# The first loads of a two-layer attention kernel: fetched once, in the order of need, with zero rows behind the first scores

## The chip, the cores and the metric

The kernel runs on one core of a Trainium2 chip. The metric is the device time of one execution in microseconds (us). Engines are named as in the profile: PE is TensorE, DVE is VectorE, ACT is ScalarE, POOL is GpSimd, SP is SyncE. SP, ACT and POOL can also issue DMAs, each from its own queue, in the order of its instructions.

## The reference

Four stages follow one another on x of 2 x 1024 tokens with 256 features, each of the form x = layernorm(x + stage(x)):

```python
# stage 1: grouped-query attention, 32 query heads, 8 key/value heads, head size 8
q, k, v = x @ Wq + bq, x @ Wk + bk, x @ Wv + bv      # 256, 64 and 64 columns
q, k = rope(q), rope(k)
att = softmax(causal(q @ k.T / sqrt(8)))              # per head, 1024 x 1024
y = (att @ v) @ Wo + bo
# stage 2: FFN with int8 weights: down(silu(gate(x)) * up(x)), 1024 hidden
# stage 3: gated delta rule, 16 heads of 128 x 128, with convolutions, gates and an output projection
# stage 4: FFN with the signs of the weights: (relu(x @ sign(up).T * up_scale) @ sign(down).T) * down_scale * output_scale
```

Only stage 1 and the loads at the start of the program are touched by the change.

## The kernel before

Matrices are multiplied in single-pass float32 (`F32R`), so each operand is split into a high part rounded to that type and a low part, the difference; `mm3` (lines 788 to 792) multiplies high by high, high by low and low by high. `sub_low` (line 738) makes a low part. A rounded high part comes either from a copy on the chip or from a DMA on POOL's queue that converts on the way.

Stage 1 works on batch b in two passes that run interleaved. `first_pass` (line 1191) projects queries and keys (`project`, line 988), applies rope by multiplying the projection and its turned copy with cosine and sine rows and adding them, splits the result and sends it through DRAM (`qds`, `kds`), from where `maxima` (line 1038) loads it in the layout of the scores: a query tile qT and a key tile kT of four groups with 32 rows each. 24 rows of a group hold parts of the heads, two take the negated row maxima later, and the others must be zero or hold a fixed pattern. `clear_rows` writes the zero rows of `qds` in DRAM (512 KB for a batch and a half of the query heads, in rows of 512 bytes, from a zeroed tile `zo`), `clear_keys` fills a key tile with the pattern `pat`. `maxima` computes scores and their row maxima; `second_pass` (line 1228) computes the scores again, exponentiates on ACT and multiplies by the values. Beside both passes `split_weights` (line 806) streams stage 3's weights through the chip and splits them: DMA on SP, high part on ACT (line 828), low part on POOL.

At the start (lines 894 to 986) the program loads the identity, four small vectors of scales and biases, the projection weights `wqkv` (704 columns) twice, once in full precision in two tiles `wf` on SP and once converted (`whi`) on POOL's queue, then for each half of batch 0's tokens x twice in the same way (`xf`, `x2h`), the rope rows, and the masks. Low parts are made on DVE. `xf` has one buffer, so the second half's load waits until the first half has been subtracted. The first key tile and one other are filled by ACT, the third by DVE; POOL clears the value and maxima tiles.

The order of the instructions on each engine is not the order of the text: a planner that works with estimated times at compile time chooses it from what is ready, by the place in the program. `after(later, earlier)` (line 794) makes an instruction come behind another in that plan, without a wait on the chip; `anchor["mm"]` is the score matmul traced last in `maxima`. Where an instruction has no such order and no inputs, it can be put far ahead of its place in the text.

Of the kernel before, what the change touches and what calls it, by code (L numbers as in the profile page):

```python
# [11 lines left out]
F32 = mybir.dt.float32  # L12
# [8 lines left out]
P = 128  # L21
B, T, E = 2, 1024, 256
NT = B * T // P
TB = T // P
HQ, HKV, D = 32, 8, 8
G = HQ // HKV
# [695 lines left out]
def tile_two_layers(ctx: ExitStack, tc: tile.TileContext, a, out):  # L722
# [5 lines left out]
    def load(pool, src, shape, dtype=F32, name=None, eng=None):  # L728
        t = pool.tile(shape, dtype, name=name, tag=name)
        (eng or nc.sync).dma_start(out=t, in_=src)  # L730
        return t
# [6 lines left out]
    def sub_low(eng, lo, full, hi):  # L738

        eng.tensor_sub(lo, full, hi)  # L740

    ident = load(const, a["c_ident"], [P, P], name="ident")
# [155 lines left out]
    nc.sync.dma_start(out=bab, in_=a["bab"])  # L898
    nc.vector.memset(zero, 0.0)
    nc.sync.dma_start(out=small[:, 4:5], in_=a["out_s"].partition_broadcast(P))  # L900
    nc.sync.dma_start(out=down_scale, in_=a["dn_s"])
    nc.vector.tensor_mul(down_scale, down_scale, small[:, 4:5].to_broadcast([P, 2]))
    nc.sync.dma_start(out=up_scale, in_=a["up_s"])
# [18 lines left out]
    def load_x(b, half):  # L922

        cols = slice(b * T + half * 512, b * T + half * 512 + 512)
        xf = work.tile([P, 2, 512], F32, name="xf", tag="xf", bufs=1)
        xh = gx.tile([P, 2, HT], F32R, name="x2h", tag="x2h")
        xl = gx.tile([P, 2, HT], F32R, name="x2l", tag="x2l")
        for d in (
            nc.sync.dma_start(out=xf, in_=xsrc[:, :, cols]), nc.gpsimd.dma_start(out=xh, in_=xsrc[:, :, cols])
        ):  # L930
            if b:
                after(d, anchor["mm"])
        for k in range(2):
            sub_low(nc.vector, xl[:, k, :], xf[:, k, :], xh[:, k, :])
        return xh, xl
# [3 lines left out]
    nc.gpsimd.dma_start(out=whi, in_=wsrc)  # L939
    for k in range(2):  # L940
        wf = work2.tile([P, NW], F32, name="wf", tag="es", bufs=4)
        nc.sync.dma_start(out=wf, in_=wsrc[:, k, :])
        sub_low(nc.vector, wlo[:, k, :], wf, whi[:, k, :])
    bqk = load(wat, a["bqk"], [P, 6], name="bqk", eng=nc.scalar)
    rope = wat.tile([P, 2, T], F32, name="rope", tag="rope")
    xcols = {0: []}
    for half in range(2):
        xcols[0].append(load_x(0, half))
        c = slice(half * 512, half * 512 + 512)
        nc.sync.dma_start(out=rope[:, :, c], in_=a["c_rope"][:, :, c])  # L950
    masks = wat.tile([P, 2, P], F32R, name="masks", tag="masks")
# [8 lines left out]
    pat = load(wat, a["c_pat"], [P, G], name="pat", eng=nc.scalar)  # L960
# [4 lines left out]
    def clear_rows(b, m):  # L965
        nc.scalar.dma_start(
            out=qds[b][m][:, :, 3 * D :, :].rearrange("k g r (n t) -> (k g) r n t", t=P),
            in_=zo.unsqueeze(1).to_broadcast([P, TB, P]),
        )

    clear_rows(0, 0)

    def clear_keys(t, copy):
        for g in range(G):
            copy(t[:, g, :], pat[:, g : g + 1].to_broadcast([P, T]))

    clear_keys(kTs[0], nc.scalar.copy)
# [7 lines left out]
    for t in mxs:  # L985
        nc.gpsimd.memset(t, -3e38)

    def project(b, m, half, xs):

        xh, xl = xs  # L990
        c0, nr = m * P, (P, P, 64)[m]
# [4 lines left out]
        for r in range(2):  # L996
            w0 = c0 + r * 320
            for k in range(2):
                n = P if r else nr
                mm3(pp[0:n, r, :], whi[:, k, w0 : w0 + n], wlo[:, k, w0 : w0 + n],  # L1000
                    xh[:, k, :], xl[:, k, :], k == 0, k == 1)
            t = work.tile([P, 512], F32, name="t", tag="t", bufs=4)
            nc.vector.scalar_tensor_tensor(
                t[0:nr], pp[0:nr, r, :], bqk[0:nr, 2 * m + r : 2 * m + r + 1], rope[0:nr, r, c], ALU.add, ALU.mult
            )
            tt.append(t)
# [159 lines left out]
    def residual(b):  # L1166

        if b == 0:
            wout["w"] = load(wout_pool, a["wo0"].rearrange("(k p) f -> p k f", p=P), [P, 2, E], name="wo0")
            wout["b"] = load_row(wout_pool, a["bo"], E, "bo")  # L1170
        after(nc.sync.dma_start(
            out=x[:, b * TB : (b + 1) * TB, :],
            in_=a["x"][b * T : (b + 1) * T, :].rearrange("(n p) e -> p n e", p=P),
        ), anchor["mm"])
        for n in range(TB):
            nc.gpsimd.tensor_add(x[:, b * TB + n, :], x[:, b * TB + n, :], wout["b"])
# [14 lines left out]
    def first_pass():  # L1191
        for b in range(B):
            if b == 0:
                for half in range(2):
                    for m in (2, 0):
                        project(b, m, half, xcols[b][half])
                    yield 0
                clear_keys(kTs[1], nc.scalar.copy)
                clear_keys(kTs[2], nc.vector.tensor_copy)
            for kv in range(HKV):  # L1200
# [9 lines left out]
                if b + 1 < B and kv >= NEXT:  # L1210
                    n, half = divmod(kv - NEXT, 2)
                    if n == 0 and half == 0:
                        xcols[b + 1] = [load_x(b + 1, h) for h in range(2)]
# [10 lines left out]
                for w in maxima(b, kv):  # L1224
                    yield w / 36
# [224 lines left out]
```

## Time and the profile before

| | |
|---|---|
| time of three runs | 2094.68 us median, 2094.62 to 2099.72 |
| the profiled execution | 2099.4 us, span 2097.7 us from its first to its last instruction |
| mean granted clock of TensorE | 0.973 |
| busy, share of the span | PE 91%, DVE 77%, ACT 54%, POOL 36% |
| DMA | 230.90 MB, mean 110 GB/s |
| first matmul of the scores | at 39.48 us |

The profile is one execution. A line of the timeline has the start in us, the duration in us, the engine, the line of the program, the operation, its output and inputs with partitions and elements, the count, and in brackets the idle time of the engine before it and what ended it. SPq and ACTq are the two engines' queues of DMA issues; the duration there is that of issuing, not of the transfer. A line of a table by stretches has, for each engine, busy time and the number of instructions, then the granted clock, the busy share of the 16 DMA engines, and GB/s.

### The profile page before, as it was taken

To read this page: it belongs to the slowest core of one execution; us is meant where nothing else is said; L and a number is where in the kernel's file an instruction comes from. 1 tells how busy PE (TensorE), PEld (TensorE's weight loads), DVE (VectorE), ACT (ScalarE), POOL (GpSimd) and SP (SyncE) were. 2 spreads that over 40 slices of the span, in tenths; PEclk is the share of its full clock that TensorE was granted. 3 is DMA by queue.
4 is the path that set the end of the run, shared out by engine and by line. 5 is a ranking of instruction groups with operands and counts; after the bars stand their busy time and mean duration, and the time that the engine had idled before them with its cause. 6 is when DMAs were issued, how large, how long until landed. Compare 5 with 4: busy or idle time off the path is not lost.

```text
span 2097.7 us, 48705 instructions
## 1 busy us (share of the span) xinstructions
PE 1905.9 (91%) x18656; PEld 1498.2 (71%) x18656; DVE 1611.1 (77%) x3878; ACT 1131.9 (54%) x2349; POOL 762.8 (36%) x1217
## 2 busy tenths in 40 slices
PE   4989999999988887899999999999999999999996
PEld 2545555555555786788888888888888888787885
DVE  5756666877747996587788878888898888978587
ACT  2355566576655345555555555655564565555543
POOL 1243333331123322144363443444345344344331
PEclk9899999999999899999999999999999999999999
DMA  7454443442132421443444444443444343443110
GB/s 222 144 164 144 144 131 126 142 134 68 51 75 61 133 64 35 127 126 91 119 121 115 124 118 115 107 120 107 121 131 119 113 118 107 137 118 107 32 41 31
DMA packets 313514, 230.90 MB, mean 110 GB/s; under 512 B 139649, under 2 KB 278657, under 8 KB 313281
## 3 DMA queue, kind: packets, MB, share of 16 engines
q1 hardware_dynamic: 299472, 210.80, 34.6%
q10 hardware_dynamic: 9632, 10.76, 1.6%
q0 software_dynamic: 4176, 6.23, 1.2%
q8 instruction: 147, 2.41, 0.5%
q14 instruction: 87, 0.70, 0.1%
HBM read 172.95 MB, written 51.87 MB: 107 GB/s over the span
## 4 chain that ended last, share of the span: by engine, by line
PE 50%; DVE 19%; ACT 6%; DMA 5%; issue 4%; SPq 1%; POOL 1%; POOLq 0%; DVEq 0%; ACTq 0%
PE pp L790 4%; PE pp L792 4%; PE pp L791 4%; PE ps L1110 4%; PE av L1131 3%; PE ps L1058 3%; DVE q L216 2%; PE pkq L404 2%; DVE at L247 2%; PE pw L529 2%; PE pm L541 2%; DVE k L216 2%; PE pkk L253 2%; PE po L555 2%; PE p L380 2%
## 5 line engine op out<-in xcount | busy, mean ns | idle before, releaser
L1067 DVE TENSOR_REDUCE mx<-ps 128x4 f32<-128x1024 f32 (+1 forms) x320 | 344.7, 1111 | 133.5 <-PE ps L1058 91.9
L1114 ACT ACTIVATE es<-ps 128x512 f32<-128x512 f32 (+1 forms) x608 | 314.8, 577 | 135.3 <-PE ps L1110 128.7
L1110 PE MATMUL ps<-qT,kT 128*128 128x512 f32 (+3 forms) x768 | 221.1, 369 | 17.9 <-ACT es L1114 15.8
L1058 PE MATMUL ps<-kT,qT 128*128 128x512 f32 x576 | 203.2, 428 | 23.3 <-DVE mx L1067 16.9
L1110 PEld LDWEIGHTS ps<-qT,kT 128*128 128x128 f32 x768 | 130.9, 189 | 106.2 <-ACT es L1114 53.7
L216 DVE SCALAR_TENSOR_TENSOR k<-pp,cw,k 128x511 f32<-128x511 f32 (+2 forms) x192 | 141.8, 740 | 31.0 <-ACT k L209 19.9
L1058 PEld LDWEIGHTS ps<-kT,qT 128*128 128x128 f32 x576 | 102.5, 194 | 85.7 <-DVE mx L1067 51.9
L1131 PE MATMUL av<-es,vaug 128*32 128x512 f32 (+3 forms) x1536 | 161.7, 501 | 0.0
L216 DVE SCALAR_TENSOR_TENSOR v<-pp,cw,v 128x511 f32<-128x511 f32 (+2 forms) x192 | 141.2, 738 | 13.1 <-ACT halos L213 8.5
L416 POOL TENSOR_TENSOR q<-q,dg 128x512 f32<-128x512 f32 x64 | 82.2, 1285 | 184.5 <-ACT pt L460 31.6
L216 DVE SCALAR_TENSOR_TENSOR q<-pp,cw,q 128x511 f32<-128x511 f32 (+2 forms) x192 | 139.2, 733 | 11.0 <-ACT q L209 9.4
L740 POOL TENSOR_TENSOR wfl<-wf,wfh 128x256 fp32r<-128x256 f32 x80 | 58.4, 733 | 208.3 <-ACT wfh L828 165.2
L1117 POOL TENSOR_SCALAR_AFFINE_SELECT es<-es 128x512 f32<-128x512 f32 x128 | 80.3, 636 | 146.9 <-ACT es L1114 146.7
L529 PE MATMUL pw<-prs,lt 128*128 128x128 f32 x512 | 84.8, 288 | 23.4 <-ACT prs L523 23.3
L555 PE MATMUL po<-wc,at 128*128 128x128 f32 x512 | 98.4, 279 | 2.1 <-ACT wc L531 1.2
L763 POOL TENSOR_TENSOR om<-om 128x8 f32<-128x8 f32 x93 | 20.3, 218 | 213.7 <-DVE om L756 113.8
L529 PEld LDWEIGHTS pw<-prs,lt 128*128 128x128 f32 x512 | 70.7, 194 | 33.2 <-ACT prs L523 29.7
L558 ACT COPY o<-po 128x256 f32<-128x256 f32 x128 | 47.6, 372 | 79.3 <-PE po L555 78.4
L242 POOL TENSOR_SCALAR_AFFINE_SELECT d<-col 128x512 f32<-128x512 f32 x64 | 51.2, 812 | 105.6 <-DVE at L247 96.7
L554 PE MATMUL po<-M,q 128*128 128x128 f32 x448 | 87.6, 278 | 0.0
L828 ACT CAST wfh<-wf 128x256 fp32r<-128x256 f32 x80 | 32.3, 406 | 101.6 <-DMA wf<-in_w1k 28.6
L531 ACT COPY wc<-pw 128x256 f32<-128x256 f32 x128 | 47.5, 371 | 72.7 <-PE pw L529 71.7
(305 smaller groups left out, 5646.1 us busy)
## 6 DMA issues: line engine op xcount, KB each, us to landing
da<-dec SPq DMA_DIRECT2D x64, 256.0 KB
wk<-w1k SPq DMA_DIRECT2D x64, 256.0 KB
wq<-w1q SPq DMA_DIRECT2D x64, 256.0 KB
wv<-w1v SPq DMA_DIRECT2D x64, 256.0 KB
dg<-dec SPq DMA_DIRECT2D x64, 256.0 KB
wg<-w1g SPq DMA_DIRECT2D x64, 256.0 KB
wo<-w1o SPq DMA_DIRECT2D x64, 256.0 KB
ad<-avs ACTq DMA_DIRECT2D x32, 256.0 KB
```

The costliest lines, as they stand in the source:

```text
L216: nc.vector.scalar_tensor_tensor(acc[:, d:], pp[:, 0 : HT - d], cw[:, n, hd, KS - 1 - d : KS - d], acc[:, d:], ALU.mult, ALU.add)
L529: nc.tensor.matmul(pw[:, r], lhsT=lt[:, h * HC + c, :], rhs=prs[:, r], start=True, stop=True)
L554: nc.tensor.matmul(po[:, r], lhsT=st[i]["q", h][:, t], rhs=M[:, r], start=True, stop=False)
L555: nc.tensor.matmul(po[:, r], lhsT=st[i]["at", h][:, t], rhs=wc[:, r], start=(M is None), stop=True)
L790: nc.tensor.matmul(out, lhsT=lhi, rhs=rhi, start=k0, stop=False)
L791: nc.tensor.matmul(out, lhsT=lhi, rhs=rlo, start=False, stop=False)
L792: nc.tensor.matmul(out, lhsT=llo, rhs=rhi, start=False, stop=k1)
L1058: anchor["mm"] = nc.tensor.matmul(ps[:, j - j0, :].rearrange("p (g k) -> p g k", k=P), lhsT=q_, rhs=kT[:, :, j * P : (j + 1) * P], start=T ...
L1067: nc.vector.tensor_reduce(mx[:, it, j0 // 2, :], ps[:, 0:n, :].rearrange("p j (g k) -> p g j k", k=P), AX.XY, ALU.max)
L1110: nc.tensor.matmul(ps[:, g - g0, :], lhsT=kT[:, g, jb * P : (jb + 1) * P], rhs=qT[:, i0 : i0 + w], start=True, stop=True,)
L1114: exps.append(nc.scalar.activation(es[:, g0 : g0 + n, 0:w], ps, AF.Exp, scale=D ** -0.5))
L1131: mm = nc.tensor.matmul(av[ROW * g : ROW * (g + 1), i0 - ih * 512 : 512], lhsT=vaugs[b][:, jb, kv, :], rhs=es[:, g, 0:w], start=(jb == 0), ...
```

## The change

Batch 0's x and the projection weights are no longer fetched a second time with conversion; their high parts are copied (and rounded) on ACT from the full-precision tiles. `load_x` and the new `load_w` issue the loads and return a function that does the splitting, which is called later. The columns of `wqkv` are arranged anew, keys and values first, and the first 192 of them come in a load of their own on ACT's queue. x is loaded first, on SP, in two pieces for a half. The second half is split when `first_pass` comes to it, behind the last rope multiplication traced before (`anchor["t"]`). The identity is loaded last. Zero rows for the first key/value head are written at the start, the others, and the loads of wo, bo and the small vectors, behind a score matmul. All three key tiles are filled by POOL, two of them behind POOL's other clearing. The product of the two scales goes from DVE to POOL.

```diff
@@ -739,7 +739,7 @@
 
         eng.tensor_sub(lo, full, hi)
 
-    ident = load(const, a["c_ident"], [P, P], name="ident")
+    ident = const.tile([P, P], F32, name="ident", tag="ident")
 
     def load_tokens(pool, n, count, bufs=1, tag="xtok"):
         t = pool.tile([P, count, E], F32, name="xtok", tag=tag, bufs=bufs)
@@ -895,12 +895,19 @@
     gx = open_pool(ctx, "gx", "right", 2)
     small = gx.tile([P, 2 * NF], F32, name="small", tag="small", bufs=1)
     bab, zero, down_scale, up_scale = small[0 : 2 * H, 0:1], small[:, 1:2], small[:, 2:4], small[:, NF:]
-    nc.sync.dma_start(out=bab, in_=a["bab"])
     nc.vector.memset(zero, 0.0)
-    nc.sync.dma_start(out=small[:, 4:5], in_=a["out_s"].partition_broadcast(P))
-    nc.sync.dma_start(out=down_scale, in_=a["dn_s"])
-    nc.vector.tensor_mul(down_scale, down_scale, small[:, 4:5].to_broadcast([P, 2]))
-    nc.sync.dma_start(out=up_scale, in_=a["up_s"])
+
+    def load_small():
+
+        for d in (
+            nc.sync.dma_start(out=bab, in_=a["bab"]),
+            nc.sync.dma_start(out=small[:, 4:5], in_=a["out_s"].partition_broadcast(P)),
+            nc.sync.dma_start(out=down_scale, in_=a["dn_s"]),
+            nc.sync.dma_start(out=up_scale, in_=a["up_s"]),
+        ):
+            after(d, anchor["mm"])
+        nc.gpsimd.tensor_mul(down_scale, down_scale, small[:, 4:5].to_broadcast([P, 2]))
+
     ones = gx.tile([H, P], F32, name="ones", tag="ones", bufs=1)
     nc.vector.memset(ones, 1.0)
     toks = open_pool(l0, "toks", "right")
@@ -925,29 +932,55 @@
         xf = work.tile([P, 2, 512], F32, name="xf", tag="xf", bufs=1)
         xh = gx.tile([P, 2, HT], F32R, name="x2h", tag="x2h")
         xl = gx.tile([P, 2, HT], F32R, name="x2l", tag="x2l")
-        for d in (
-            nc.sync.dma_start(out=xf, in_=xsrc[:, :, cols]), nc.gpsimd.dma_start(out=xh, in_=xsrc[:, :, cols])
-        ):
-            if b:
-                after(d, anchor["mm"])
-        for k in range(2):
-            sub_low(nc.vector, xl[:, k, :], xf[:, k, :], xh[:, k, :])
-        return xh, xl
+        if b:
+            after(nc.sync.dma_start(out=xf, in_=xsrc[:, :, cols]), anchor["mm"])
+            after(nc.gpsimd.dma_start(out=xh, in_=xsrc[:, :, cols]), anchor["mm"])
+        else:
+            for k in range(2):
+                nc.sync.dma_start(out=xf[:, k, :], in_=xsrc[:, k, cols])
+
+        def split():
+            for k in range(2):
+                if b == 0:
+                    d = nc.scalar.copy(xh[:, k, :], xf[:, k, :])
+                    if half:
+                        after(d, anchor["t"])
+                sub_low(nc.vector, xl[:, k, :], xf[:, k, :], xh[:, k, :])
+            return xh, xl
+
+        return split
 
     whi = wat.tile([P, 2, NW], F32R, name="whi", tag="whi")
     wlo = wat.tile([P, 2, NW], F32R, name="wlo", tag="wlo")
-    nc.gpsimd.dma_start(out=whi, in_=wsrc)
-    for k in range(2):
-        wf = work2.tile([P, NW], F32, name="wf", tag="es", bufs=4)
-        nc.sync.dma_start(out=wf, in_=wsrc[:, k, :])
-        sub_low(nc.vector, wlo[:, k, :], wf, whi[:, k, :])
-    bqk = load(wat, a["bqk"], [P, 6], name="bqk", eng=nc.scalar)
     rope = wat.tile([P, 2, T], F32, name="rope", tag="rope")
-    xcols = {0: []}
-    for half in range(2):
-        xcols[0].append(load_x(0, half))
+
+    def load_w(c, eng):
+        wf = work2.tile([P, 2, c.stop - c.start], F32, name="wf", tag="es", bufs=4)
+        eng.dma_start(out=wf, in_=wsrc[:, :, c])
+
+        def split():
+            nc.scalar.copy(whi[:, :, c], wf)
+            sub_low(nc.vector, wlo[:, :, c], wf, whi[:, :, c])
+
+        return split
+
+    def load_rope(half):
         c = slice(half * 512, half * 512 + 512)
         nc.sync.dma_start(out=rope[:, :, c], in_=a["c_rope"][:, :, c])
+
+
+    split_x = load_x(0, 0)
+    split_w = load_w(slice(0, 192), nc.scalar)
+    load_rope(0)
+    bqk = load(wat, a["bqk"], [P, 6], name="bqk", eng=nc.scalar)
+    pat = load(wat, a["c_pat"], [P, G], name="pat", eng=nc.scalar)
+    split_w()
+    xcols = {0: [split_x()]}
+    split_w = load_w(slice(192, NW), nc.sync)
+    split_w()
+    xcols[0].append(load_x(0, 1))
+    load_rope(1)
+    nc.sync.dma_start(out=ident, in_=a["c_ident"])
     masks = wat.tile([P, 2, P], F32R, name="masks", tag="masks")
     nc.gpsimd.dma_start(out=masks, in_=a["c_mask"])
 
@@ -957,24 +990,26 @@
     kTs = [big.tile([P, G, T], F32R, name=f"kT{i}", tag=f"kT{i}") for i in range(NKT)]
     zo = wat.tile([P, P], F32, name="zo", tag="zo")
     nc.vector.memset(zo, 0.0)
-    pat = load(wat, a["c_pat"], [P, G], name="pat", eng=nc.scalar)
     qds = [[dram.tile([4, G, ROW, T], F32, name=f"qd{b}{i}", tag=f"qd{b}{i}") for i in range(2)] for b in range(B)]
     ads = [[dram.tile([4, G, ROW, T], F32, name=f"ad{b}{i}", tag=f"ad{b}{i}") for i in range(2)] for b in range(B)]
     kds = [dram.tile([HKV, 3 * D, T], F32, name=f"kd{b}", tag=f"kd{b}") for b in range(B)]
 
-    def clear_rows(b, m):
-        nc.scalar.dma_start(
-            out=qds[b][m][:, :, 3 * D :, :].rearrange("k g r (n t) -> (k g) r n t", t=P),
-            in_=zo.unsqueeze(1).to_broadcast([P, TB, P]),
+    def clear_rows(b, m, kvs=slice(0, 4)):
+        n = (kvs.stop - kvs.start) * G * (ROW - 3 * D)
+        d = nc.scalar.dma_start(
+            out=qds[b][m][kvs, :, 3 * D :, :].rearrange("k g r (n t) -> (k g) r n t", t=P),
+            in_=zo[0:n].unsqueeze(1).to_broadcast([n, TB, P]),
         )
-
-    clear_rows(0, 0)
-
-    def clear_keys(t, copy):
+        if "mm" in anchor:
+            after(d, anchor["mm"])
+
+    clear_rows(0, 0, slice(0, 1))
+
+    def clear_keys(t):
         for g in range(G):
-            copy(t[:, g, :], pat[:, g : g + 1].to_broadcast([P, T]))
-
-    clear_keys(kTs[0], nc.scalar.copy)
+            nc.gpsimd.tensor_copy(t[:, g, :], pat[:, g : g + 1].to_broadcast([P, T]))
+
+    clear_keys(kTs[0])
     vaugs = [big.tile([P, TB, HKV, ROW], F32, name=f"vaug{i}", tag=f"vaug{i}") for i in range(B)]
     for t in vaugs:
         nc.gpsimd.memset(t, 0.0)
@@ -984,23 +1019,25 @@
     mxs = [wat.tile([P, TB, TB // 2, G], F32, name=f"mx{i}", tag=f"mx{i}") for i in range(NMX)]
     for t in mxs:
         nc.gpsimd.memset(t, -3e38)
+    for t in kTs[1:]:
+        clear_keys(t)
 
     def project(b, m, half, xs):
 
         xh, xl = xs
-        c0, nr = m * P, (P, P, 64)[m]
+        c0, nr = (192, 448, 0)[m], (P, P, 64)[m]
 
         c = slice(half * 512, half * 512 + 512)
         tt = []
         pp = ps_s.tile([P, 2, 512], F32, name="pp", tag="s")
         for r in range(2):
-            w0 = c0 + r * 320
+            w0 = c0 + r * nr
             for k in range(2):
                 n = P if r else nr
                 mm3(pp[0:n, r, :], whi[:, k, w0 : w0 + n], wlo[:, k, w0 : w0 + n],
                     xh[:, k, :], xl[:, k, :], k == 0, k == 1)
             t = work.tile([P, 512], F32, name="t", tag="t", bufs=4)
-            nc.vector.scalar_tensor_tensor(
+            anchor["t"] = nc.vector.scalar_tensor_tensor(
                 t[0:nr], pp[0:nr, r, :], bqk[0:nr, 2 * m + r : 2 * m + r + 1], rope[0:nr, r, c], ALU.add, ALU.mult
             )
             tt.append(t)
@@ -1166,8 +1203,11 @@
     def residual(b):
 
         if b == 0:
-            wout["w"] = load(wout_pool, a["wo0"].rearrange("(k p) f -> p k f", p=P), [P, 2, E], name="wo0")
-            wout["b"] = load_row(wout_pool, a["bo"], E, "bo")
+            wout["w"] = wout_pool.tile([P, 2, E], F32, name="wo0", tag="wo0")
+            wout["b"] = wout_pool.tile([P, E], F32, name="bo", tag="bo")
+            after(nc.sync.dma_start(out=wout["w"], in_=a["wo0"].rearrange("(k p) f -> p k f", p=P)), anchor["mm"])
+            after(nc.sync.dma_start(out=wout["b"], in_=a["bo"].partition_broadcast(P)), anchor["mm"])
+            load_small()
         after(nc.sync.dma_start(
             out=x[:, b * TB : (b + 1) * TB, :],
             in_=a["x"][b * T : (b + 1) * T, :].rearrange("(n p) e -> p n e", p=P),
@@ -1192,11 +1232,11 @@
         for b in range(B):
             if b == 0:
                 for half in range(2):
+                    if half:
+                        xcols[b][half] = xcols[b][half]()
                     for m in (2, 0):
                         project(b, m, half, xcols[b][half])
                     yield 0
-                clear_keys(kTs[1], nc.scalar.copy)
-                clear_keys(kTs[2], nc.vector.tensor_copy)
             for kv in range(HKV):
                 if kv == 1 and b == 0:
                     clear_rows(b, 1)
@@ -1210,7 +1250,7 @@
                 if b + 1 < B and kv >= NEXT:
                     n, half = divmod(kv - NEXT, 2)
                     if n == 0 and half == 0:
-                        xcols[b + 1] = [load_x(b + 1, h) for h in range(2)]
+                        xcols[b + 1] = [load_x(b + 1, h)() for h in range(2)]
                     if n < 2:
                         if half == 0:
                             clear_rows(b + 1, n)
@@ -1221,7 +1261,9 @@
                         else:
                             project(b + 1, 1, half, xs)
                             values(b + 1, half)
-                for w in maxima(b, kv):
+                for n, w in enumerate(maxima(b, kv)):
+                    if n == 0 and b == 0 and kv == 0:
+                        clear_rows(0, 0, slice(1, 4))
                     yield w / 36
                 yield 0
 
@@ -1408,7 +1450,7 @@
     arrays = {
         "x": x,
         "xT": x.T,
-        "wqkv": np.concatenate([wq, wk, turned(wq), turned(wk), l0("attn_Wv")], axis=1),
+        "wqkv": np.concatenate([wk, turned(wk), l0("attn_Wv"), wq[:, :P], turned(wq)[:, :P], wq[:, P:], turned(wq)[:, P:]], axis=1),
         "bqk": np.stack([bq[:P], turned(bq)[:P], bq[P:], turned(bq)[P:], pad(bk), np.concatenate([turned(bk), l0("attn_bv")])], axis=1),
         "wo0": l0("attn_Wo"),
         "bo": l0("attn_bo"),
```

## The prediction

> **What bounds the kernel now.** I read the page's head, then busy time by stretches, then the stretch 0 to 50 us in order of time, the waits of the DMA queues, and the DMA issues with their sizes. By stretches (busy us of each engine, granted clock, DMA share, GB/s):
>
> ```profile
> 0.00:20.00 20.00, 1.09 (x2) 0.39 (x2) 10.03 (x11) 8.94 (x9) 7.42 (x15) 1.00 0.92 274
> 20.00:40.00 20.00, 14.19 (x48) 9.32 (x49) 12.38 (x19) 3.85 (x6) 0.00 (x0) 1.00 0.54 183
> 40.00:50.00 10.00, 4.65 (x15) 2.44 (x14) 6.53 (x7) 0.26 (x1) 0.00 (x0) 0.94 0.66 179
> 50.00:60.00 10.00, 8.63 (x18) 4.41 (x17) 8.11 (x8) 0.74 (x3) 1.45 (x2) 0.50 0.76 241
> 100.00:200.00 100.00, 89.59 (x481) 49.76 (x484) 60.88 (x72) 55.52 (x116) 38.56 (x52) 0.98 0.45 141
> ```
>
> The kernel is a TensorE kernel (PE busy 91% of 2097.7 us) with an idle head: PE does 1.09 us of work in its first 20 us, while the DMA engines are 92% busy. Later it is 90% busy and more. The head in order of time:
>
> ```profile
> 10.32 4.17 ACTq L966 DMA_DIRECT2D qd<-zo  x2
> 14.04 0.38 SPq L929 DMA_DIRECT2D xf<-in_xT  x1
> 19.72 1.29 DVE L740 TENSOR_TENSOR x2l<-xf,x2h 128x512 fp32r<-128x512 f32 x2 [4.70 <-DMA xf<-in_xT]
> 20.46 0.69 PE L791 MATMUL pp<-x2l,whi 128*64 128x512 f32 x1 [8.23 <-DVE x2l L740]
> 25.50 1.29 DVE L740 TENSOR_TENSOR x2l<-xf,x2h 128x512 fp32r<-128x512 f32 x2 [0.58 <-DMA xf<-in_xT]
> 39.48 0.47 PE L1058 MATMUL ps<-kT,qT 128*128 128x512 f32 x1 [2.32 <-DMA qT<-qd]
> 49.25 2.04 PE L1058 MATMUL ps<-kT,qT 128*128 128x512 f32 x4 [3.77 <-DMA qT<-qd]
> ```
>
> The first projection waits for the low part of x (20.46), that for the full-precision copy of x (xf), and xf is only issued at 14.04. Why so late is in the DMA queue's own waits (us in total, times, longest), and what was in its way in the issues (count, KB each, us to landing):
>
> ```profile
> SPq L929 <- DMA qd<-zo: 7.9, 1, 7.9
> ```
>
> ```profile
> qd<-zo ACTq DMA_DIRECT2D x4, 512.0 KB
> x2h<-in_xT POOLq DMA_DIRECT2D x2, 512.0 KB, 9.9
> whi<-in_wqkv POOLq DMA_DIRECT2D x1, 704.0 KB, 6.4
> ```
>
> All four writes of zero rows (2048 KB) have been put at the very front, and xf stands behind one of them. With x and the weights fetched twice (x2h 1024, xf 1024, whi 704, wf 704), rope 1024, wo 256, masks and bo 128 each and ident 64, some 7.1 MB go out before 25 us. The microseconds 6 to 24 move 325 to 406 GB/s each; that is the head: 7.3 MB at about 370 is 19.7 us.
>
> **Part 1, loads up to the first low part.** Before it is done at 19.72 + 0.69 = 20.41 us. In the new order only half of x (512 KB) and 192 columns of weights (192 KB) must land, 0.72 MB or 1.9 us at 370 GB/s. The fixed part: the 2 KB of pat, issued at 1.25, landed at 3.35, so 2.1 us. Issue at 0.81 as now, plus 2.1, plus 1.9 is 4.8. The other bound is xf's own trip among other traffic, 5.6 us from 14.04: 0.81 + 0.4 for a second issue + 5.6 = 6.8. I take 5.8. The high parts are now rounded on ACT: 406 ns for 256 columns (wfh) and 620 for 512 (hi) put 384 at about 0.51, and x's first half at 0.62; with DVE's 0.69 for the low part this gives 5.8 + 0.51 + 0.62 + 0.69 = 7.6. ACT's table load (1.28) fits before the landing. **Gain 12.8 us** (11.8 to 13.8).
>
> **Part 2, from there to the first scores.** Before 39.48 - 20.41 = 19.1 us of projection, rope, splitting, and the trip through DRAM. That chain stays, but the second half's subtraction (1.29 at 25.50, after 0.58 of idling for xf) is now ordered behind the first half's rope multiplications. **Gain 1.9** (0 to 1.9). The second half keeps its place: its loads want the xf buffer free (about 8.3 us) and 4.5 us as now (issue at 21.04, subtraction at 25.50), so they land near 13, and its projections begin when the first half's are through. rope's first half and the remaining 512 KB of weights are issued behind x, and at 370 GB/s they add 2.8 us, to about 8.6: before the first rope product, which needs twelve matmuls at 0.43 after 6.9.
>
> **Part 3, what is added on GpSimd.** The patterns of the three key tiles (8 copies on ACT at 1.04, 4 on DVE) become 12 copies on GpSimd. Its nearest row is a cast of 128x512 in 612 ns, so 1.22 each, 14.7 us in all, beside memsets of 4.5 us that it does already. With pat landing at about 4.5, even the whole list ends near 24; the first key tile is written at about 34.18 - 13 = 21 and its four copies take 4.9. So GpSimd's own time is covered. Its neighbour is not: these rows (min/median/max ns first) show VectorE held by GpSimd:
>
> ```profile
> L1081 DVE TENSOR_TENSOR mp<-nm,mp x16: 187/200/426, 70.5 to 598.9; 128x32 fp32r<-128x32 f32 x16
> 70.12 0.73 POOL L740 TENSOR_TENSOR wfl<-wf,wfh 128x256 fp32r<-128x256 f32 x1 [3.06 <-ACT wfh L828]
> 70.48 0.43 DVE L1081 TENSOR_TENSOR mp<-nm,mp 128x32 fp32r<-128x32 f32 x1
> L975 DVE CAST kT<-pat x4: 675/680/5740, 3.3 to 10.2; 128x1024 fp32r<-128x1024 f32 x4
> ```
>
> The subtraction that takes 200 ns took 426 and ended with GpSimd's instruction (70.85 against 70.91); the cast of 680 took 5740 while GpSimd cleared memory. In the new head VectorE does eight two-input operations up to the first scores (two for weights, two for x, two sums, two low parts), so 0 to 8 x 1.22 = 9.8 us of waiting. Four lie on the chain (x twice, the queries' sum and low part), and an arrival in the middle of a copy waits half of it: 4 x 0.61. **Loss 2.4** (0 to 9.8).
>
> The Trainium skill (SBUF — State Buffer, section with the port table and "The single rule") speaks against the change here: a VectorE instruction with two inputs in SBUF and a GpSimd instruction that reads SBUF exclude each other for the whole instruction, while one that only writes does not. Taken at its word for all eight, each losing a full copy, the sum below would be a gain of 3.4 instead of 10.8; the row at 70.48 agrees with it for one case.
>
> **Part 4, what is moved into the running kernel.** Zero rows, three writes of 512 KB and one of 384, go to ACT's queue among the exponentials; ACT's busy share there is 56%. The nearest issue rows are 1.34 for two when the DMA engines are free (at 1.75 us) and 4.17 for two when full (10.32); bo's held the queue for 5.84. At the DMA share of 0.45 I take 0.65 each, 2.6 on ACT. In 40 to 200 us PE waits on ACT for 4.8 us only, so less than half arrives: **loss 1.0** (0 to 23.4 = 4 x 5.84). What is queued behind are exponentials, and PE's second pass waits for those. Four small loads (0.33 to 0.43 each), wo and bo go to SP behind the first scores, near the load of x at 103 us: SP idles 53 us for ACT's casts in 40 to 200, and wo is first read at 385 us, bo at 108.61 by GpSimd, which already waits 2.1 us for x there. Nothing. ident (first read at 72) and masks: nothing. The product for down_scale goes from DVE to GpSimd and waits there for its loads, with selects behind it that feed PE: **loss 0.5** (0 to 2.1, the fixed part of a load).
>
> **Sum.** -12.8 - 1.9 + 2.4 + 1.0 + 0.5 = -10.8 us. The profiled execution took 2099.4 us (span 2097.7 and 1.7 around it), 4.7 over the median of 2094.68 and inside the three runs (2094.62 to 2099.72). So 2088.6 for such an execution, and **2083.9** for the median. The gain can travel to the end, since nothing after the head has a date of its own: the weight stream, scores and exponentials start from the first scores. The instruction order is planned at compile time and can shift with the head; PE's idle time in 100 to 600 us is 31.7 us (10.4 + 15.7 + 5.6), and a third of it, 10 either way, is my estimate of that risk.
>
> **Rivals.**
> 1. *The head stays long for another reason.* VectorE loses every meeting with GpSimd (9.8): a gain of 3.4, 2091.3. For it: the cast of 5.74 us. Against: four of eight operations are off the chain and GpSimd also waits in its turn.
> 2. *Slower, by zero rows on ACT's queue.* If each issue is held like bo's, 23.4 us instead of 1.0 gives -11.8 + 23.4 = +11.6, 2106.3. It decides from 4.5 us an issue on (18.1 in all, +6.3). For it: the share of 0.76 in 50 to 60 us, and 512-byte rows. Against: 0.45 after 100 us.
> 3. *More is gained, by the clock.* In 50 to 60 us the granted clock is 0.50 (0.54 in 60 to 70), after PE idled 3.77 us at 49.25. VectorE is busy 8.11 and 8.26 of 10 there, so an unthrottled PE could give at most 3.6: 2080.3; with the planner's order on its side, 2072. For it: a smaller gap between the halves. Against: the second half still makes the same trip through DRAM. The Trainium skill (TensorE: Matmul & The Clock Gate, Part 1) has idle time of some 3.4 us put the clock at half. By that rule 0.4 us off the gap would be enough for this case.
> 4. *It doesn't do what it says:* the planner again puts zero rows in front of x. Then nothing is won in part 1 beyond the removed 1728 KB (4.8 us): 2090. The orders behind the score matmul speak against it. I count this with rival 1.
>
> **Chances.** A measurement of this kernel can tell about 0.3%, 6.3 us, from no change: faster is below 2088.4, slower above 2101.0. Forecast case 0.56; rival 3 (more) 0.16; rivals 1 and 4 (same) 0.17; rival 2 (slower) 0.11. So faster 0.72, same 0.17, slower 0.11. The range goes from rival 3's 2072 to 2096, which takes in rivals 1 and 4 with 5 us of planner's noise and leaves out rival 2 and a small tail below.
>
> **What would show it.** Right: xf issued at about 0.8; the first low part near 7.6; first scores near 27 (39.48 - 12.3) and the second half's near 37; the zero rows on ACT's queue after the first scores, each issue under 1 us; VectorE's subtractions in the head at 0.7 to 1.9 us; PE in 100 to 200 us (shifted by 11) still near 90%. Wrong: subtractions of 2 us and more (rival 1); issues of zero rows over 4.5 us with PE waiting on ACT behind them (rival 2); a head that is 11 us shorter with the end in its old place, which would mean that a later wait took it back.

## The result, and the profile after

| | before | changed |
|---|---|---|
| median of six runs each, us | 2094.65 (2091.54 to 2099.72) | 2115.83 (2107.58 to 2123.76) |
| ratio, 95% interval | | 1.0097, 1.0077 to 1.0116 |
| the profiled execution, us | 2099.4 | 2123.76 (span 2122.0) |
| mean granted clock | 0.973 | 0.962 |
| first scores, at us | 39.48 | 31.01 |

The changed kernel is 21 us slower; 11 us faster were forecast. Yet its head is shorter, by 8.5 us at the first scores (12.3 were predicted). Below are the stretches of the changed kernel (length; busy us and instructions of PE, PE's weight loads, DVE, ACT and POOL; granted clock; DMA share; GB/s). The last one runs from the first product of stage 3's keys and queries (called "stage 3's keys" below) to the last matmul of stage 4's first layer:

```profile
0.00:20.00 20.00, 10.18 (x25) 6.18 (x25) 7.90 (x12) 6.32 (x9) 18.12 (x23) 0.96 0.52 164
20.00:40.00 20.00, 12.96 (x39) 7.17 (x37) 14.71 (x19) 2.54 (x4) 1.33 (x2) 0.84 0.44 136
40.00:50.00 10.00, 3.81 (x8) 2.17 (x8) 2.87 (x3) 0.40 (x1) 0.72 (x1) 0.50 0.88 240
100.00:200.00 100.00, 93.42 (x544) 54.70 (x545) 64.00 (x74) 60.91 (x126) 44.28 (x60) 0.97 0.55 172
725.00:2109.20 1384.20, 1272.48 (x14924) 1120.33 (x14922) 1081.08 (x3108) 726.64 (x1538) 540.04 (x895) 0.97 0.35 100
```

The same stretch of the kernel before, whose code the change does not touch there:

```profile
738.60:2084.70 1346.10, 1250.71 (x14937) 1101.41 (x14935) 1087.88 (x3104) 728.33 (x1543) 539.02 (x895) 0.98 0.37 103
```

PE works 10.18 us in the first 20 instead of 1.09, and 93.42 in 100 to 200 us instead of 89.59. The changed kernel reaches stage 3's keys at 725.0 instead of 738.6, 13.6 us ahead, and then needs 1384.2 us instead of 1346.1 for the rest: 38.1 lost. 13.6 - 38.1 is -24.5, which is the difference of the two profiled executions (24.4; they lie 7.9 and 4.7 us above their medians). Of the 38 us, about 22 are longer busy time of PE (1272.48 against 1250.71) and 16 more idling. The head of the changed kernel in order of time:

```profile
0.81 0.87 SPq L940 DMA_DIRECT2D xf<-in_xT  x2
6.01 0.69 DVE L740 TENSOR_TENSOR x2l<-xf,x2h 128x512 fp32r<-128x512 f32 x1
7.14 14.18 POOL L1010 CAST kT<-pat 128x1024 fp32r<-128x1024 f32 x12 [0.76 <-DMA pat<-in_c_pat]
7.70 0.80 SPq L940 DMA_DIRECT2D xf<-in_xT  x2
10.05 1.04 ACT L962 CAST whi<-wf 128x1024 fp32r<-128x1024 f32 x1 [3.09 <-DMA wf<-in_wqkv]
11.14 0.80 PE L790 MATMUL pp<-x2h,whi 128*128 128x512 f32 x1 [1.99 <-ACT whi L962]
15.74 1.26 DVE L1052 TENSOR_TENSOR t<-t 64x512 f32<-64x512 f32 x1
17.57 1.14 ACT L945 CAST x2h<-xf 128x512 fp32r<-128x512 f32 x2
20.75 1.11 DVE L740 TENSOR_TENSOR x2l<-xf,x2h 128x512 fp32r<-128x512 f32 x1
30.15 0.81 ACTq L999 DMA_DIRECT2D qd<-zo  x1
31.01 0.39 PE L1095 MATMUL ps<-kT,qT 128*128 128x512 f32 x1
45.72 2.04 PE L1095 MATMUL ps<-kT,qT 128*128 128x512 f32 x4 [7.92 <-DMA qT<-qd]
```

In the way of x stood four writes of zero rows and the second copies. What goes out in the first 110 us now (count, KB each), with x at the size of a piece and each thing once:

```profile
xf<-in_xT SPq DMA_DIRECT2D x4, 256.0 KB
...
wf<-in_wqkv SPq DMA_DIRECT2D x1, 512.0 KB
...
wf<-in_wqkv ACTq DMA_DIRECT2D x1, 192.0 KB
```

and the one wait of SP's queue for the loads of x, by the second half for its buffer:

```profile
SPq L940 <- DVE x2l L740: 1.5, 1, 1.5
```

x is issued at 0.81 without waiting for anything, the first low part is done at 6.70, and the first scores start at 31.01. The second half's scores start only 3.5 us earlier than before (45.72 against 49.25), after PE idled 7.92 us instead of 3.77.

And the waits of PE that grew most in the stretch after 725 us, in the changed kernel (us in total, times, longest; px and pm are results of stage 3's matmuls):

```profile
PE px L335 <- issue: 16.4, 9, 5.2
PE pm L541 <- ACT wc L531: 15.7, 34, 0.8
```

and in the kernel before:

```profile
PE pm L541 <- ACT wc L531: 10.2, 22, 0.7
PE px L335 <- issue: 4.0, 3, 1.7
```

No wait of the list is put down to a load, a zero row or a scale that the change has moved. Copies of stage 3 on ACT end the waits of pm; for those of px the profile shows no releaser ("issue"). The program has been planned in another order there. By operation, tiles and sizes in the two traces, only 22% of VectorE's sequences of six successive instructions from stage 3's keys on occur in both (86% of PE's, 30% of ACT's).

### The profile page after: what moved, and what is told of

It reads as the page before. It is cut to its first block, busy times and chain, and to the rows that moved or that the text cites. A ratio compares the mean times of both kernels' runs of the same rounds, so it can differ in the third digit from the quotient of the medians.

```text
span 2122.0 us, 48753 instructions
## 1 busy us (share of the span) xinstructions
PE 1923.7 (91%) x18656; PEld 1516.2 (71%) x18656; DVE 1592.0 (75%) x3873; ACT 1129.3 (53%) x2347; POOL 777.1 (37%) x1227
## 5 line engine op out<-in xcount | busy, mean ns | idle before, releaser
L1095 PE MATMUL ps<-kT,qT 128*128 128x512 f32 x576 | 203.8, 428 | 24.5 <-DVE mx L1104 15.0
L216 DVE SCALAR_TENSOR_TENSOR k<-pp,cw,k 128x509 f32<-128x509 f32 (+2 forms) x192 | 142.1, 741 | 36.6 <-ACT k L209 17.4
L216 DVE SCALAR_TENSOR_TENSOR v<-pp,cw,v 128x511 f32<-128x511 f32 (+2 forms) x192 | 141.7, 739 | 12.3 <-ACT halos L213 7.3
L541 PE MATMUL pm<-wc,kc 128*128 128x128 f32 x448 | 75.1, 291 | 15.8 <-ACT wc L531 15.7
L478 DVE TENSOR_TENSOR xtok<-pf,xtok 128x512 f32<-128x512 f32 x64 | 43.7, 683 | 59.8 <-PE pf L792 53.2
L790 PE MATMUL pf<-wo,yh 128*128 128x256 f32 x256 | 80.0, 312 | 7.7 <-DVE xtok L478 6.1
```

Source lines behind the costliest of these rows:

```text
L216: nc.vector.scalar_tensor_tensor(acc[:, d:], pp[:, 0 : HT - d], cw[:, n, hd, KS - 1 - d : KS - d], acc[:, d:], ALU.mult, ALU.add)
L541: nc.tensor.matmul(pm[:, r], lhsT=st[i]["kc", h][:, c, :], rhs=wc[:, r], start=True, stop=True)
L790: nc.tensor.matmul(out, lhsT=lhi, rhs=rhi, start=k0, stop=False)
L1095: anchor["mm"] = nc.tensor.matmul(ps[:, j - j0, :].rearrange("p (g k) -> p g k", k=P), lhsT=q_, rhs=kT[:, :, j * P : (j + 1) * P], start=T ...
```

## The experiments

Two theories. **Order:** any edit at the start makes the planner re-order all that follows, and the order it happens on in stage 3 decides the time. **Head:** something in the change itself (zero rows, GpSimd's patterns, the later split, the clock) costs the 21 us, and stage 3 is only where it shows. To tell them apart, an order is held: the planned order of one program is written as a table into another, and each engine's instructions from there on are chained to it. The chains carry no semaphore (`NoSync`), since an engine's instructions follow one another anyway. That holding an order costs little of itself is seen below: e5, which holds e4's order, takes 2079.21 us against e4's 2076.86. The table `d` has the orders of PE, DVE, ACT, POOL and SP one behind the other.

```diff
+    tail = traced[-PLAN_N:]
+    at = 0
+    for n in PLAN_LENS:
+        order = np.cumsum(d[at : at + n]).tolist()
+        at += n
+        for a, b in zip(order, order[1:]):
+            tc.add_manual_dep(
+                tail[b], tail[a].name,
+                mybir.DependencyInfo(mybir.DependencyClass.NoSync, mybir.DependencyReason.DATA), reason="order",
+            )
...
         tile_two_layers(tc, aps, out)
+        pin(tc)
```

### The orders exchanged

`e1` is the changed kernel with the order of the kernel before from about 100 us on (the last 20,700 instructions; two of these, writes of zero rows, are left free):

> The changed kernel, with the last 20,700 traced instructions (all from the third key/value head of batch 0 on, about 100 us) held on every engine in the order that the plan of the kernel before has for them; only the zero rows are left free. Theory 'plan': the change itself gains 8 to 14 us in the head and keeps it, and what is lost is the order that the planner made of the untouched third stage. Then about 2094.7 - 11 = 2083 (2079 to 2088). Rival 'execution': the moved loads or the placement of the data make the later stages slower whatever their order. Then it stays near 2115. In between, 2095 to 2105: both.

`e2` is the kernel before with the order of the changed one, from about 450 us on (the last 18,000 instructions):

> The kernel before, with its last 18,000 traced instructions (from about 450 us on) held in the order that the plan of the changed kernel has for them. No load is changed. Theory 'plan': the third stage loses what it lost in the changed kernel, some 30 to 38 us, so about 2125 to 2135. Rival 'execution': 2095, as the loads are those of before.

| | median, us | ratio to before, 95% | first scores | stage 3's keys | from there to the end of stage 4's first layer |
|---|---|---|---|---|---|
| before | 2094.7 | | 39.5 | 738.6 | 1346.1 |
| changed | 2115.8 | 1.0097 (1.0077 to 1.0116) | 31.0 | 725.0 | 1384.2 |
| e1 | 2094.27 | 0.9997 (0.9981 to 1.0013) | 30.1 | 736.2 | 1346.9 |
| e2 | 2129.48 | 1.0156 (1.0122 to 1.0189) | 39.7 | 736.4 | 1381.8 |

The stretch from stage 3's keys on, first of e1, then of e2:

```profile
736.20:2083.10 1346.90, 1248.84 (x14937) 1100.36 (x14936) 1088.68 (x3104) 728.35 (x1543) 538.34 (x895) 0.98 0.37 103
```

```profile
736.40:2118.10 1381.70, 1267.59 (x14924) 1115.45 (x14922) 1079.61 (x3108) 726.19 (x1538) 539.16 (x895) 0.97 0.36 100
```

and PE's waits in it in e2, which are the changed kernel's almost one by one:

```profile
PE px L335 <- issue: 15.9, 9, 4.1
PE pm L541 <- ACT wc L531: 15.7, 34, 0.7
```

The loss goes with the order and not with the loads: the old loads with the new order lose it, the new loads with the old order do not. In the traces VectorE's sequences of six from stage 3's keys on are those of the kernel before in e1 and those of the changed kernel in e2, all of them. Second finding: e1's head is 9.4 us ahead at the first scores, and nothing of it is left in the time. By its interval, what the head is worth at this order lies between -4 and +3 us.

### Another order by an edit of no cost

If the order is a matter of luck, a tiny edit must move the time as well. In `e3` (kernel before) and `e4` (changed kernel) one memset of 0.17 us, of the tile of zeros, goes to GpSimd; nothing is held.

```diff
-    nc.vector.memset(zo, 0.0)
+    nc.gpsimd.memset(zo, 0.0)
```

> The kernel before with one edit that costs nothing by itself: the clearing of the tile of zeros (0.17 us on VectorE) is done by GpSimd. Theory 'plan': the order of the third stage is made anew (6 of 10 short sequences of VectorE's instructions there differ), and the time is moved by 5 to 30 us, more likely up. Rival 'execution': 2095 within 3.

> The changed kernel with the same edit: the tile of zeros cleared by GpSimd. Theory 'plan': another order, another time, 5 to 30 us from 2115, either way; first scores still near 31 us. Rival 'execution': 2115 within 5.

e3: 2104.46 us (ratio 1.0049, 1.0026 to 1.0071), 10 slower than before. e4: 2076.86 us (0.9907, 0.9878 to 0.9936), 39 faster than the changed kernel, and with that the changed kernel wins 18. Their stretches from stage 3's keys on are 1352.7 and 1343.5 us. In stages 1 and 2 e4's order is the changed kernel's to 99%; from stage 3's keys on they share 28% of VectorE's sequences of six. Is it the memset or the order? `e5` is the changed kernel, unchanged, with e4's order held; `e6` has the loads of before with the same order:

> The changed kernel, nothing of it undone, with its last 20,700 traced instructions (from about 100 us on) held in the order that the plan of e4 has. Theory 'plan': the changed kernel with a good order of the third stage takes e4's time, 2077 (2073 to 2083), with 1343 us from the first matmul of the third stage's keys to the last matmul of the second FFN instead of 1384. Rival 'the memset's engine itself mattered': near 2115.

> The kernel before, loads as they were, in the same order of e4 from about 100 us on. It gives the worth of the new head with the order taken out: theory 'the head is worth 9 us' (first scores 40.3 against 30.7): 2086. If the head is worth what e4 shows against the kernel before (18): 2095. If nothing: 2077.

| | median, us | ratio to before, 95% | first scores | second half's | end of row maxima no. 32 | stage 3's keys |
|---|---|---|---|---|---|---|
| e5, new loads | 2079.21 | 0.9926 (0.9908 to 0.9945) | 29.9 | 43.3 | 89.3 | 721.6 |
| e6, old loads | 2076.57 | 0.9914 (0.9897 to 0.9930) | 40.0 | 49.5 | 91.0 | 722.1 |

Row maxima no. 32 is the 32nd instruction on VectorE that reduces scores to row maxima (`mx`).

It is the order. The same program takes 2115.8 or 2079.2 us, and the program before 2094.7, 2129.5 or 2076.6. The lead of 13.6 us at stage 3's keys, too, was the order's: e6 has it with the old loads. And again the new loads bring nothing at an equal order (+2.6 us, with intervals that overlap), although the first scores come 10.1 us earlier.

Where does the head's lead go? It is 6.2 us at the second half's scores and 1.7 at the 32nd row maxima. The stretches 50 to 70 us of e5, then of e6, then 50 to 60 us of e4:

```profile
50.00:60.00 10.00, 8.90 (x18) 4.19 (x17) 8.40 (x9) 1.21 (x3) 2.14 (x3) 0.50 0.58 164
60.00:70.00 10.00, 9.11 (x38) 6.69 (x39) 7.02 (x12) 1.02 (x2) 2.02 (x2) 0.88 0.22 68
```

```profile
50.00:60.00 10.00, 7.84 (x18) 4.04 (x17) 8.09 (x8) 0.81 (x2) 1.45 (x2) 0.65 0.85 244
60.00:70.00 10.00, 7.93 (x29) 4.73 (x29) 8.57 (x11) 1.18 (x3) 2.17 (x3) 1.00 0.38 118
```

```profile
50.00:60.00 10.00, 6.93 (x22) 3.12 (x21) 9.77 (x10) 0.81 (x2) 1.85 (x3) 1.00 0.69 191
```

The first half's scores are soon used up; PE then idles 6.1 us for the second half's queries to come back from DRAM (in e6 3.5), and works on at a granted clock of 0.50 and 0.88 where e6 has 0.65 and 1.00. But e4, whose head is e5's but for the memset and which also idles 6.1 us there, has 1.00 from 50 us on. Its 32nd row maxima end at 86.1, 4.9 us before e6's, and its time is still e6's (2076.86 and 2076.57). So what is left of the lead at this point scatters by 3 us from one profile to another, and that the clock takes part of it is argued, not shown. At stage 3's keys e5 is 0.5 us ahead of e6, e4 3.7, and e1 2.4 ahead of the kernel before. The medians can't tell a rest of that size from nothing at the end; the 10.8 that was forecast they exclude. The Trainium skill (TensorE: Matmul & The Clock Gate, Part 1) states that an idle window of about 3.4 us puts the clock at half; the 7.92 us of idling and the granted clock of 0.50 that follows in the changed kernel agree with it.

### The parts of the change one by one, at an equal order

All of these hold e4's order, so they are read against e5. `e8` gives the patterns back to ACT and VectorE:

```diff
-    def clear_keys(t):
+    def clear_keys(t, copy):
...
-            nc.gpsimd.tensor_copy(t[:, g, :], pat[:, g : g + 1].to_broadcast([P, T]))
...
+            copy(t[:, g, :], pat[:, g : g + 1].to_broadcast([P, T]))
+
+    clear_keys(kTs[0], nc.scalar.copy)
...
+                clear_keys(kTs[1], nc.scalar.copy)
+                clear_keys(kTs[2], nc.vector.tensor_copy)
```

> The changed kernel in e4's order, with the patterns of the key tiles filled by ACT and VectorE as in the kernel before. Theory 'GpSimd's copies hold VectorE': the sums and low parts of the head are back at 0.69 us and the first scores come 1 to 3 us earlier than 31. Rival: ACT, which now rounds the high parts, is late by its 8 copies of 1.04, and the first scores come 2 to 6 us later. Time: as e5 with that shift, within 3.

`e9` writes the zero rows in front again (`clear_rows(0, 0)` whole, without its order):

```diff
-        if "mm" in anchor:
-            after(d, anchor["mm"])
...
-    clear_rows(0, 0, slice(0, 1))
...
+    clear_rows(0, 0)
...
-                    if n == 0 and b == 0 and kv == 0:
-                        clear_rows(0, 0, slice(1, 4))
```

> The changed kernel in e4's order, with all zero rows of the first half written at the start again and the other three writes free to be put there by the planner. My step 1: 2 MB more ahead of x, 5 to 6 us at 370 GB/s, so first scores at 34 to 37 and the time 4 to 6 us over e5. Rival: written in 512-byte rows from ACT's queue they hardly delay x, which is on SP's: less than 2 us.

`e10` fetches the high parts a second time with conversion, as before, all else being new:

```diff
+            nc.gpsimd.dma_start(out=xh, in_=xsrc[:, :, cols])
...
-                    d = nc.scalar.copy(xh[:, k, :], xf[:, k, :])
...
+        nc.gpsimd.dma_start(out=whi[:, :, c], in_=wsrc[:, :, c])
...
-            nc.scalar.copy(whi[:, :, c], wf)
```

> The changed kernel in e4's order from about 100 us on, but with the high parts of x and of the weights fetched by converting DMAs on GpSimd's queue again (1728 KB more), in the new order of loads. My step 1: first scores 2 to 5 us later than 31. What e5 and e6 say (2079.2 and 2076.6 with first scores at 30.7 and 40.8): whatever the head, the end does not move: 2076 to 2081.

`e11` splits the second half of x at once, not behind the first half's rope:

```diff
-                    if half:
-                        after(d, anchor["t"])
...
-    xcols[0].append(load_x(0, 1))
+    split_x = load_x(0, 1)
     load_rope(1)
+    xcols[0].append(split_x())
...
-                    if half:
-                        xcols[b][half] = xcols[b][half]()
```

> The changed kernel in e4's order from about 100 us on, with the second half of x split as soon as it has landed, not behind the first half's rope multiplications. Theory 'the second half sets the pace': its scores, at 45.7 in the changed kernel and at 49.3 before, come at 40 to 43, the first scores up to 2 us later, and 2 us or more are still seen in the maxima 100 us on; the end moves by less than its scatter (2075 to 2080). Rival 'the trip through DRAM and SP's queue set it': the second half's scores stay within 1.5 us of 45.7.

| | median, us | ratio to before, 95% | first scores | second half's | end of row maxima no. 32 |
|---|---|---|---|---|---|
| e11 | 2072.96 | 0.9900 (0.9883 to 0.9916) | 30.3 | 43.5 | 85.5 |
| e5 | 2079.21 | 0.9926 (0.9908 to 0.9945) | 29.9 | 43.3 | 89.3 |
| e9 | 2077.26 | 0.9919 (0.9901 to 0.9937) | 32.9 | 46.0 | 90.0 |
| e8 | 2080.45 | 0.9942 (0.9919 to 0.9965) | 31.2 | 46.0 | 90.0 |
| e6 | 2076.57 | 0.9914 (0.9897 to 0.9930) | 40.0 | 49.5 | 91.0 |
| e10 | 2088.89 | 0.9972 (0.9957 to 0.9986) | 47.8 | 58.1 | 97.1 |

Neither the zero rows nor the patterns are worth anything that can be told apart at the end. With the zero rows in front (e9) the first scores come 3.0 us later than e5's. Without GpSimd's copies (e8) the sums and low parts are back at 0.68 us, but ACT, behind its own copies, rounds the rest of the weights at 14.45 instead of 9.62 us, and the first scores come 1.3 us later. The table is in the order of the 32nd row maxima: e10's 7.8 us there are still seen in the time, while e6 and e5, 10 us apart at the first scores, can't be told apart at the end. e11 has the best time of all and beats both kernels. That this is e11's edit is not shown: its interval overlaps e5's, and the 3.8 us by which its 32nd row maxima come before e5's are nearly e4's 3.2.

The second half's scores start in e11 where e5's do, although the half is rounded at 13.12 instead of 17.02 us. SP's queue takes the difference. There the write of the second half's queries stands behind the load of a key tile, which waits until the keys of that half have gone to DRAM; first e5's wait, then e11's:

```profile
SPq L1084 <- DMA kd<-hi: 2.6, 1, 2.6
```

```profile
SPq L1083 <- DMA kd<-lo: 4.1, 1, 4.1
```

The high part of the queries is ready at 32.70 us in e5 and at 30.26 in e11, but the write is issued at 34.93 and 35.27.

e10 shows what GpSimd can do to VectorE. Both subtractions of the low part (min/median/max ns), then the neighbours in order of time:

```profile
L740 DVE TENSOR_TENSOR x2l<-xf,x2h x2: 677/6963/13249, 8.2 to 21.4; 128x512 fp32r<-128x512 f32 x2
```

```profile
8.91 8.91 POOL L1007 CAST kT<-pat 128x1024 fp32r<-128x1024 f32 x9
17.94 3.00 POOL L1007 CAST kT<-pat 128x1024 fp32r<-128x1024 f32 x3
21.54 0.69 PE L791 MATMUL pp<-x2l,whi 128*64 128x512 f32 x1 [9.57 <-DVE x2l L740]
```

A subtraction that takes 0.68 us elsewhere starts at 8.2 and lasts 13.25, through all twelve pattern copies; PE's matmul that needs it starts at 21.54, 0.6 us after the last copy has ended (20.94). Neither expectation for e10 came true: the first scores were to come 2 to 5 us late and come 17.9 us after e5's, and the end was not to move. The order in e10 differs from e5's only in the head, and the 7.8 us of difference in the 32nd maxima become 9.7 at the end.

### Two of these in their own order

`e12` is e8's program and `e13` e9's, with nothing held:

> The kernel of e8 (patterns filled by ACT and VectorE) without e4's order: the planner's own. Its head is e8's. If the order of the later stages is what is being measured, it is 5 to 40 us away from e8's 2080.5, and the difference arises after 700 us. If the head decides: within 4 of it.

> The kernel of e9 (zero rows at the front) without e4's order: the planner's own. As for e12: 5 to 40 us away from e9's 2077.3 by the order alone, with the difference arising after 700 us; within 4 of it if the head decides.

e12 takes 2109.65 us (ratio 1.0081, 1.0060 to 1.0103) and 1367.7 from stage 3's keys on; with e4's order it took 2080.45. e13 takes 2092.54 (1.0003, 0.9985 to 1.0021) and 1353.0; held, 2077.26. Read alone, e13 would have said that the zero rows' new place costs 23 us, and e12 that the patterns' place costs 6. At an equal order both are within 2 us of e5. So a part that is undone without holding the order measures the planner.

## Why the prediction was wrong

**The step that failed** is the risk that was set beside the sum and counted as nothing in it. The planner's order was put at 10 either way, from PE's 31.7 idle us between 100 and 600 us, and left out of the sum. The changed kernel takes 2094.27 us in the order of before (e1) and 2115.83 in its own: the order costs 21.6 where 0 was summed. It was also looked for in the wrong place. In its own order each program has its own length from stage 3's keys on: 1343.5 (e4), 1346.1 (before), 1352.7 (e3), 1353.0 (e13), 1367.7 (e12), 1384.2 us (changed). That is a spread of 41 us, from edits that all lie in the head. In the seven programs that run in e4's order (e4, e5, e6, e8 to e11) it is 1337.2 to 1344.2. The bound came from the stretch next to the change; it should have come from the longest stretch planned after it. None of the four rivals had this mechanism at this size; the one on the slower side blamed the zero rows.

**"The gain can travel to the end" also failed.** At an equal order it is -0.4 us (e1 against before) and +2.6 (e5 against e6) instead of -10.8. With the order's 21.6 this -0.4 makes up the 21.2 us that were measured. The argument was that nothing after the head has a date of its own. But the second half of the queries has one: it still goes through rope and DRAM, in SP's queue behind a load that waits for the keys, and the first half's scores do not last until then. That takes some 4 of the 10 us (e5 against e6: 10.1 at the first scores, 6.2 at the second half's); where the rest goes is open. e10 shows that the head is not free to grow, either.

- **Part 1, first low part:** 7.6 predicted, 6.70 measured, and xf issued at 0.81 as said. Right.
- **Part 2, first scores and second half:** 27 and 37 predicted, 31.0 and 45.7 measured. The rest of the weights was put at 8.6 and came near 10, so PE waited 1.99 us at 11.14. From the first low part to the first scores it takes 24.3 us; 19.6 were predicted (19.1 - 1.9 + 2.4). The larger miss is the second half: its x was issued at 7.70 as expected, it was rounded only at 17.57, behind the rope multiplications, and PE idled 7.92 us before its scores. The prediction booked this order as a gain of 1.9. The late rounding is not what holds the second half: e11 rounds early, and SP's queue keeps its scores where they were.
- **Part 3, GpSimd's patterns:** 1.22 each predicted, 14.18 / 12 = 1.18 measured. VectorE's loss was put at 2.4; the summing of 64x512 took 1.26 instead of 0.67, a subtraction 1.11 instead of 0.69, wlo some 0.26 too long: 1.3 in all, about half of what was put down. Whether any of it lies on the path is not shown: e8 is free of it, but there ACT is late instead. The worst case, 9.8, was not the end of it: 12.6 us in e10. The Trainium skill (SBUF — State Buffer, "The single rule") says that the one that issues first holds the shared ports for a whole instruction while the other blocks. The measurement goes further: an instruction recorded as started 0.67 us before the copies was kept out by twelve of them in a row, not by one (one profile).
- **Part 4, zero rows:** 0.65 an issue predicted. The four that were moved start at 30.15 (0.9 us before the first scores, since the order stands only in the plan), 52.24, 126.75 and 213.50, and take 0.81, 0.63, 0.58 and 0.57. The profile of the changed kernel has (min/median/max ns of all five, the 1.33 being the one at the start):

```profile
L999 ACTq DMA_DIRECT2D qd<-zo x5: 569/632/1334, 5.0 to 213.5; - x5
```

Right, and the slower rival, which needed 4.5 us an issue, is refuted; e9 adds that their place is worth less than can be measured at the end. The scales' product on POOL was not tested by itself.
- **The clock (the rival on the faster side):** the other way round. The gap before the second half grew, and the throttled stretch came earlier instead of vanishing (0.50 in 40 to 50 us, 0.94 before). In e4 it is over by 50 us, and its time is no better than e6's.

**What stays open:** why one order of stage 3 is better than another. PE's waits of px put down to "issue" rise in the same order as the six lengths above: 0.9 us in e4, then 4.0, 6.3, 6.5, 8.1 and 16.4 in the changed kernel. Those of pm are 10.2 to 10.5 us in the two shortest and 14.7 to 15.7 in the others; the granted clock is lower (0.97 against 0.98) only in the changed kernel's order. But no run isolates one wait. The case is shown for the order as a whole.

## What to carry to other kernels

Where a planner orders the whole program at compile time, an edit anywhere draws a new order for all that follows: compare two versions with the order held beyond the edit, and bound that risk by the longest stretch planned after it (here 41 us of 2095), not by the idle time next door. Follow a shortened head to a later milestone, at which both paths must have arrived, before counting it; the first scores said 8 to 10 us, the 32nd row maxima 2 to 5, the end nothing that could be measured. When the order is what decides, drawing several and keeping the best is a measure of its own: it gave 18 us here with no gain from the loads at all (e6).

## What the runs showed of the hardware that was not expected

- A VectorE operation with two SBUF inputs can be kept out by a run of GpSimd copies for the whole run: 13.25 us for an operation of 0.68 (e10, one profile). With the copies placed only a little differently against the subtractions, the same twelve copies cost 1.3 us in all (the changed kernel).
- The same 14,900 matmuls in another order take 1272.5 instead of 1250.7 us of PE's busy time, at a granted clock of 0.97 instead of 0.98 (the changed kernel and the kernel before, from stage 3's keys on).
